# A graph layer's messages held back at the changes of transformer layer, the last block's q moved, and the projection's copies put first on ACT

## The chip, the cores and the metric

The kernel runs on one core of one Trainium2 chip. The metric is the device time of one execution in microseconds (us); the time of a version is the median of its runs. A separate execution is taken by the hardware profiler, and all views come from that one. TensorE is called PE in the views, VectorE DVE, ScalarE ACT, GpSimd POOL; SP issues most of the DMAs.

## The reference

All is fp32. There are 3125 nodes of 256 features and 100,000 edges, sorted by target node (`dst`). Cut to what matters:

```
xn  = layernorm(x)                                   # 3125 x 256
gnn = normalize(relu([xn, h_N] @ W2.T))              # row norm 1
      h_N = segment_sum(relu([xn[src], edge_attr] @ W1.T + b1), dst)
mix = xn; four times:
      h = layernorm(mix)*g1 + b1
      q = softmax(h @ Wq, within a head), k = softmax(h @ Wk, over the nodes), v = h @ Wv
      mix += (q @ (k.T @ v)) @ Wo + bo               # 8 heads of 32
      mix += gelu(layernorm2(mix) @ W1 + b1) @ W2 + b2   # 1024 wide
x   = x + gnn + mix
out = layernorm-ed top-2-of-16 mixture of experts on layernorm(x), plus x
```

The softmax of k runs over all nodes. So k.T @ v of a layer is known only when the last node has been seen, and no q @ (k.T @ v) can start before that: this is what is called a change of layer below.

## The kernel before, in words

The 3125 nodes are 25 tiles of 125 rows (`t`), in 7 blocks of 4, 4, 4, 4, 4, 3 and 2 tiles (`BLOCKS`). All of x stays on the chip as `xm`.

**Prologue** (0 to 126 us). For each block: normalize x (`stage_xn`), scale its rows for layer 0 on ACT (`stage_xh1`, L379, one ACT copy for each tile), transpose it on PE and copy that out on ACT (`stage_xnT`, copy in L389), multiply it with the message weights (`stage_proj`, L399) and write this projection to a table `proj` in memory. Beside that runs the first half of layer 0.

**First half of a layer, by blocks**: `stage_t1` transposes the normalized rows (`hT`); `stage_k` (matmul L432) keeps a running maximum over the nodes (L434, `neg` L443) and takes exponentials on ACT; `stage_q` (matmul L458) is the softmax within heads: maximum `qm` L464, subtraction L465 and, after ACT's exponential, sum L467, reciprocal L468, product L469 on DVE; `stage_ek` and `stage_qT` transpose both (L480, L144), and `stage_m` (L495) adds the block's k.T @ h to `msum`, rescaled on DVE.

**Change of layer**: `context` divides `msum` (`mean`, L516), transposes it (`meanT`, L521, with scale and shift half on ACT, half on DVE), multiplies with Wv (`ctx`, L528; masked on DVE) and Wo (`mo`, L537, L538). `stage_y` (L547) then adds q @ mo to `xm` block by block, with the statistics of the second layernorm; `stage_ln2` normalizes (`xh`, L122) and adds b2 on POOL (L563); `stage_t2` transposes it (`h2T`, L144).

**Second half, by blocks**: `stage_f1` (L581, gelu on ACT) and `stage_f2` (L591). The next layer's k, q, ek, qT and m of block b−1 follow f2 of block b, so that only the last two blocks' are left when the last f2 is done.

**Messages.** 784 chunks of 128 edges make 98 groups of 8. A group has three kinds of steps. Kind 0, `load_chunk`: one indirect DMA on POOL (L255) gathers 128 rows of the table; the first chunk of a group also loads the edge attributes `ea` on SP. Kind 2, `message_step`: 16 matmuls for the attributes (`pw`, L294), four additions on DVE (L298), four relus on ACT (L299), and a matrix `hot` of targets on DVE (L301). Kind 1, `sum_step`: 16 matmuls that sum the group by target (`pq`, L279), a copy on ACT (`osb`, L282), and for the group before two transposes (`win`, L270) that are added to `hNT` (L273).

The steps lie in one list `due`, each with a place: kind 1 of group g at g, kind 2 at g + 0.5, the gathers up to 1.25 groups (`LEAD`) ahead of use. They are mixed into layers 0 to 2: each piece of the transformer's work calls `worked(columns)` (L324) with its number of matmul columns. That advances `place` and emits each step that has come due, a gather after a tiny copy (`tick`, L334) on POOL that waits for that piece of work:

```
place += columns * (NG + 1 + LEAD) / total
while due and due[-1][0] <= place:
    _, kind, step, i = due.pop()
```

`total` is 579,330 columns, so a group is emitted every 5779. `spread` turns this on in the prologue's last blocks. In `context` and after `stage_y` of blocks 0 and 1, five further calls `worked(12 * D)` stand, which are no work of the transformer.

The instructions of PE, ACT and POOL are executed in the order of the program text; those of DVE and SP in an order that a scheduler chose when the kernel was built.

**Last layer.** After layer 2 a branch (L804) chooses another way for targets far apart, which this input doesn't take. Then come the loads of w2x and w2n (L813), and the update of the nodes (`stage_g`, matmuls L617 and L620, squares `sq` L625) is mixed into `context` of the last layer through the same three `worked(12 * D)` calls. Routing and the experts follow.

Of the kernel before, what the change touches and what calls it, by code (L numbers as in the profile page):

```python
# [8 lines left out]
F32 = mybir.dt.float32  # L9
# [8 lines left out]
D = 256  # L18
P = 128
TP = 125  # L20
NT = N // TP
KC = D // P
# [10 lines left out]
DEPTH = 4  # L33
# [6 lines left out]
BT = 4  # L40
# [24 lines left out]
def gps_layer(ctx: ExitStack, tc: tile.TileContext, a, out):  # L65
# [60 lines left out]
    with ExitStack() as ph:  # L126
# [189 lines left out]
        NB = len(BLOCKS)  # L316
        attention = NT * (KC * D + 2 * KC * TP + 3 * KC * P + KC * (D + 1))
        forward = NT * (KC * D + KC * P + NF * KC * TP + NF * D)
        total = (DEPTH - 1) * (attention + forward + 60 * D)
        place = -LEAD  # L320
        spread = False
        tick = tmp.tile([1, 1], F32, name="tick")

        def worked(columns, mark=None):  # L324


            nonlocal place
            if not spread:
                return
            place += columns * (NG + 1 + LEAD) / total  # L330
            while due and due[-1][0] <= place:
                _, kind, step, i = due.pop()
                if kind == 0 and mark is not None:
                    nc.gpsimd.tensor_copy(tick, mark)  # L334
                    mark = None
                step(i)

        def affine(dst, ps, l, which):
            nc.scalar.activation(dst[:, 0, :], ps[:, 0, :], AF.Identity,  # L339
# [18 lines left out]
        def stage_xn(b):  # L358
            r = BLOCKS[b]
            n = len(r)  # L360
            for t in r:
                stats(tmp, xm[:, t, :], t)
            rs = tmp.tile([TP, 3, 2, BT], F32, name="rs", bufs=3)
            st["rs", b] = rs
            v = mv[:, r[0]:r[-1] + 1, 1]
            if n < BT:
                nc.vector.memset(rs[:, 0], 1.0)
            nc.vector.tensor_scalar(rs[:, 0, 0, :n], v, EPS, None, op0=ALU.add)
            nc.vector.scalar_tensor_tensor(rs[:, 0, 1, :n], rs[:, 0, 0, :n], EPS, v, op0=ALU.mult, op1=ALU.add)
            nc.vector.tensor_mul(rs[:, 0, 1, :n], rs[:, 0, 1, :n], rs[:, 0, 0, :n])  # L370
            rsqrt(rs[:, 1], rs[:, 0], rs[:, 2])
            for i, t in enumerate(r):
                nc.vector.tensor_scalar(xm[:, t, :], xm[:, t, :], mv[:, t, 0:1], rs[:, 1, 0, i:i + 1],
                                        op0=ALU.subtract, op1=ALU.mult)
            nc.vector.tensor_mul(rs[:, 2, 0, :], rs[:, 0, 0, :], rs[:, 1, 1, :])
# [129 lines left out]

        def context(l):
            nonlocal mo
            bo = tmp.tile([P, D], F32, name="bo")  # L510
            nc.sync.dma_start(bo, rows_bcast(a["mix_bo"][l], P))
            mean = tmp.tile([P, KC, D], F32, tag="pj", name="mean", bufs=2)
            ksr = tmp.tile([P, KC], F32, name="ksr")
            nc.vector.reciprocal(ksr, msum[:, :, D])
            for c in range(KC):
                nc.vector.tensor_scalar(mean[:, c, :], msum[:, c, :D], ksr[:, c:c + 1], None, op0=ALU.mult)  # L516
            worked(12 * D)
            ps = mm_tile("meanT_ps").rearrange("p (h m) -> p h m", h=KC)
            for h in range(KC):
                for c in range(KC):  # L520
                    nc.tensor.transpose(ps[:, h, c * P:(c + 1) * P], mean[:, c, h * P:(h + 1) * P], ident)  # L521
            meanT = tmp.tile([P, KC, D], F32, tag="pj", name="meanT", bufs=2)
            affine(meanT, ps, l, 0)
            worked(12 * D)
            ps = mm_tile("ctx_ps")[:, :D].rearrange("p (c m) -> p c m", c=KC)
            for c in range(KC):
                for h in range(KC):
                    nc.tensor.matmul(ps[:, c, :], wt["Wv"][:, h, c * P:(c + 1) * P],  # L528
                                     meanT[:, h, c * P:(c + 1) * P],
                                     start=(h == 0), stop=(h == KC - 1))  # L530
            ctxT = tmp.tile([P, KC, P], F32, name="ctxT")
            nc.vector.tensor_mul(ctxT, ps, bmask[:, None, :].to_broadcast([P, KC, P]))
            worked(12 * D)
            ps = mm_tile("mo_ps").rearrange("p (c d) -> p c d", c=KC)
            mo = tmp.tile([P, KC, D], F32, name="mo")
            for c in range(KC):
                nc.tensor.matmul(ps[:, c, :], ctxT[:, c, :], wt["Wo"][:, c, :], start=True, stop=True)  # L537
            nc.vector.scalar_tensor_tensor(mo, bo[:, None, :].to_broadcast([P, KC, D]), 1.0 / HEADS, ps,  # L538
                                           op0=ALU.mult, op1=ALU.add)


        def stage_y(l, b):
# [110 lines left out]
        with tc.manual_schedule(engines=in_order):  # L653

            prepared = windows()
            stage_xn(0)
            stage_xh1(0)
            stage_xnT(0)
            stage_proj(0)
            stage_xn(1)  # L660
            stage_t1(0, 0)
            for b in range(NB + 1):
                if b < NB:
                    stage_k(0, b)
                    if b + 2 < NB:
                        stage_xn(b + 2)
                    stage_q(0, b)
                if b > 1:
                    next(prepared, None)
                if b > 0:  # L670
                    stage_m(0, b - 1)
                if b + 1 < NB:
                    stage_xh1(b + 1)
                    stage_xnT(b + 1)
                    if b > 1:
                        next(prepared, None)
                    stage_proj(b + 1)
                    stage_t1(0, b + 1)
                if b < NB:
                    if b > 1:  # L680
                        next(prepared, None)
                    stage_ek(0, b)
                    stage_qT(0, b)
                if b == NB - 2:
                    for _ in prepared:
                        pass
                    spread = True
            for l in range(last):
                start_layer(l)
                context(l)  # L690
                load(l + 1, "Wk", "Wq", "Wv")
                stage_y(l, 0)
                stage_ln2(0)
                stage_y(l, 1)
                worked(12 * D)
                stage_t2(l, 0)
                worked(12 * D)
                for b in range(NB):
                    stage_f1(l, b)
                    if b > 1:  # L700
                        stage_ek(l + 1, b - 2)
                        stage_qT(l + 1, b - 2)
                    if 0 < b < NB - 1:
                        stage_y(l, b + 1)
                    if b > 1:
                        stage_m(l + 1, b - 2)
                    if b > 0:
                        stage_t1(l + 1, b - 1)
                    if b + 1 < NB:
                        stage_ln2(b + 1)  # L710
                    stage_f2(l, b)
                    stage_stats(b)
                    if b > 0:
                        stage_k(l + 1, b - 1)
                    if b + 1 < NB:
                        stage_t2(l, b + 1)
                    if b > 0:
                        stage_q(l + 1, b - 1)
                    stage_ln1(b)
                stage_ek(l + 1, NB - 2)  # L720
                stage_qT(l + 1, NB - 2)
                stage_t1(l + 1, NB - 1)
                stage_m(l + 1, NB - 2)
                stage_k(l + 1, NB - 1)
                stage_q(l + 1, NB - 1)
                stage_ek(l + 1, NB - 1)
                if l + 1 < last:
                    stage_qT(l + 1, NB - 1)
                    stage_m(l + 1, NB - 1)
            while due:  # L730
                _, _, step, i = due.pop()
                step(i)
            stage_qT(last, NB - 1)
            stage_m(last, NB - 1)

        def any_order():
            table = dram.tile([ROWS, D], F32, name="table")
# [70 lines left out]
        edges_only.close()  # L808
        gates = ph.enter_context(tc.tile_pool(name="gates", bufs=1))
        w2x = wts.tile([P, KC, D], F32, tag="wk", name="w2x")  # L810
        w2n = wts.tile([P, KC, D], F32, tag="wq", name="w2n")
        for w, k in ((w2x, 0), (w2n, D)):
            nc.sync.dma_start(w, a["gnn_W2"][k:k + D].rearrange("(c p) n -> p c n", p=P))  # L813
        gw = gates.tile([P, KC, E], F32, name="gw")
# [117 lines left out]
        with tc.manual_schedule(engines=in_order - {mybir.EngineType.Pool}):  # L932
            start_layer(last)
            load_update(0)
            load_update(1)
            parts = [(0, slice(0, 1)), (0, slice(1, 2)), (1, slice(0, 1))]

            def worked(columns, mark=None):
                if columns == 12 * D and parts:
                    stage_g(*parts.pop(0))  # L940

            context(last)
            stage_y(last, 0)
            stage_ln2(0)
            add_update(0)
            stage_g(1, slice(1, 2))
# [319 lines left out]
```

## Time and profile before

| | us |
|---|---|
| median of 3 runs (lowest, highest) | 2221.84 (2219.28, 2224.5) |
| profiled execution | 1994.73 |
| span in its trace | 1993.0 |
| last projection to first f1 of layer 0 | 126.8 to 179.2 |
| last f2 of layer 0 to first f1 of layer 1 | 529.2 to 595.8 |
| last f2 of layer 1 to first f1 of layer 2 | 942.7 to 1014.7 |
| last f2 of layer 2 to first f1 of layer 3 | 1362.7 to 1418.8 |

The times in all views are counted from the start of the span. The profiled execution is 11% shorter than the runs, and 1.7 us longer than its span. A row of a view names the engine, the line of the kernel and the tiles (out<-in); a wait is put down to the instruction whose end released it.

### The profile page before, as it was taken

The numbers are of one execution on the slowest core, as the hardware profiler recorded it, in microseconds if no ns is written. First come the engines' busy times: TensorE is split into PE (matmuls) and PEld (weight loads), VectorE is DVE, ScalarE is ACT, GpSimd is POOL, SyncE is SP. The second block draws the span as 40 slices with busy tenths as digits, with TensorE's granted clock in tenths as the row PEclk, the third lists the DMA queues.
The fourth block names the chain that finished last, engine by engine and source line by source line (L and its number), as shares of the span: only waits on it lengthen the run. The fifth ranks groups of instructions, "written<-read, shape, count | busy, mean of one in ns | idle before, by whom it ended". The sixth has DMA issues, their size and how long they took to land. (4 is left out here: it accounts for less than half of the span.)

```text
span 1993.0 us, 30766 instructions
## 1 busy us (share of the span) xinstructions
PE 1807.7 (91%) x9749; PEld 1269.3 (64%) x9749; DVE 1165.1 (58%) x3761; ACT 743.6 (37%) x1343; POOL 1126.5 (57%) x1429
## 2 busy tenths in 40 slices
PE   6988999999888999999889999998999994999963
PEld 4764656666655666667546666666777783888841
DVE  7654566666664666766656666765646653333326
ACT  3543444344533444544333444443222231222202
POOL 1026777677667777777677777771114435545512
PEclk9998999999988999999889999999999996999987
DMA  6123333233433233334423233333211113777744
GB/s 188 66 77 92 89 85 88 79 88 93 129 98 91 84 93 91 89 84 127 118 81 89 85 90 87 89 89 100 67 29 29 28 19 116 241 259 260 273 130 120
DMA packets 83294, 210.74 MB, mean 106 GB/s; under 512 B 26523, under 2 KB 42306, under 8 KB 78389
## 3 DMA queue, kind: packets, MB, share of 16 engines
q0 software_dynamic: 44800, 118.16, 20.6%
q1 hardware_dynamic: 37246, 87.31, 13.9%
q10 hardware_dynamic: 1078, 3.20, 0.6%
q8 instruction: 84, 1.38, 0.3%
q14 instruction: 86, 0.70, 0.1%
HBM read 187.34 MB, written 21.19 MB: 105 GB/s over the span
## 5 line engine op out<-in xcount | busy, mean ns | idle before, releaser
L255 POOL DMA_INDIRECT gat<-proj,src_i x784 | 761.9, 972 | 212.4 <-issue 163.4
L581 PE MATMUL f_ps<-h2T,ww 128*128 128x500 f32 (+2 forms) x896 | 360.6, 551 | 6.4 <-ACT h2T L339 5.8
L299 ACT ACTIVATE gat<-gat 128x512 f32<-128x512 f32 x392 | 237.6, 630 | 341.0 <-DVE gat L298 315.4
L591 PE MATMUL f_ps<-ww,gT 128*125 128x256 f32 x1600 | 362.3, 382 | 0.0
L298 DVE TENSOR_TENSOR gat<-gat,pw 128x512 f32<-128x512 f32 x392 | 245.5, 680 | 162.1 <-PE pw L294 138.3
L591 PEld LDWEIGHTS f_ps<-ww,gT 128*125 128x125 f32 x1600 | 295.1, 188 | 58.4 <-issue 10.5
L581 PEld LDWEIGHTS f_ps<-h2T,ww 128*128 128x128 f32 x896 | 167.0, 192 | 168.5 <-issue 122.8
L583 ACT ACTIVATE gT<-f_ps,ffb 128x500 f32<-128x500 f32 (+2 forms) x224 | 135.6, 631 | 136.4 <-PE f_ps L581 135.8
L279 PE MATMUL pq<-gat,hot 128*32 128x256 f32 x1568 | 137.6, 405 | 22.4 <-ACT gat L299 22.3
L273 DVE TENSOR_TENSOR hNT<-hNT,win_ps 128x64 f32 x392 | 84.7, 216 | 74.4 <-PE win_ps L270 64.4
L925 POOL DMA_INDIRECT slots<-rec,at x50 | 59.5, 1189 | 110.0 <-DVE rs_u L113 63.7
L596 DVE TENSOR_TENSOR xm<-xm,f_ps 125x512 f32<-125x512 f32 (+1 forms) x52 | 34.7, 667 | 138.7 <-PE f_ps L591 136.4
L1120 PE MATMUL e_ps<-ew,hs 128*128 128x256 f32 x464 | 112.8, 381 | 2.2 <-DVE o L1124 2.2
L294 PE MATMUL pw<-w1w,ea 4*128 4x256 f32 x1568 | 114.6, 403 | 0.0
L1127 POOL DMA_INDIRECT outs<-o,ids x58 | 57.4, 989 | 100.6 <-DVE o L1125 97.5
L458 PE MATMUL q_ps<-wwq,hT 128*125 128x256 f32 x400 | 99.8, 402 | 4.6 <-DVE gat L298 3.6
L563 POOL TENSOR_TENSOR xm<-xm,b 125x1024 f32<-125x1024 f32 (+2 forms) x28 | 59.9, 2140 | 77.6 <-DVE xh L122 58.5
L547 PE MATMUL y_ps<-mo,qT 128*125 128x256 f32 x400 | 98.0, 397 | 4.9 <-DVE mo L538 4.9
L294 PEld LDWEIGHTS pw<-w1w,ea 4*128 4x128 f32 x1568 | 72.5, 185 | 45.0 <-issue 34.5
L495 PE MATMUL m_ps<-xh,ek 125*128 125x257 f32 x400 | 97.9, 398 | 1.8 <-ACT ek L481 1.8
L279 PEld LDWEIGHTS pq<-gat,hot 128*32 128x32 f32 x1568 | 49.6, 112 | 77.9 <-ACT gat L299 45.3
L1120 PEld LDWEIGHTS e_ps<-ew,hs 128*128 128x128 f32 x464 | 85.2, 190 | 20.4 <-issue 4.5
(222 smaller groups left out, 2652.8 us busy)
## 6 DMA issues: line engine op xcount, KB each, us to landing
ew<-ffn_w SPq DMA_DIRECT2D x37, 1154.0 KB
gat<-proj,src_i POOLq DMA_INDIRECT x784
ww<-mix_W SPq DMA_DIRECT2D x8, 1024.0 KB
ea<-eaT SPq DMA_DIRECT2D x392, 4.0 KB
ogs<-outs SPq DMA_DIRECT2D x6, 448.0 KB
ogs<-outs ACTq DMA_DIRECT2D x6, 448.0 KB
out<-ogs SPq DMA_DIRECT2D x6, 448.0 KB
xnT_d<-stage SPq DMA_DIRECT2D x5, 500.0 KB
```

Source lines behind the costliest of these rows:

```text
L255: nc.gpsimd.indirect_dma_start(out=gats[-1][:, (j // SC) % 2, j % SC, :], out_offset=None, in_=proj, in_offset=bass.IndirectOffsetOnAxis(a ...
L279: nc.tensor.matmul(pq[s * W:(s + 1) * W, :], hot[:, s * SC + i, :], gats[s // 2][:, s % 2, i, :], start=(i == 0), stop=(i == SC - 1))
L294: nc.tensor.matmul(pws[s][:, i, :], ea[s * W:s * W + 4, i * P:(i + 1) * P], w1w[s * W:s * W + 4, :], start=True, stop=True)
L298: nc.vector.tensor_add(msg, msg, pws[s])
L299: nc.scalar.activation(msg, msg, AF.Relu)
L458: nc.tensor.matmul(ps[:, i, :], hT[:, c, cols(o + i)], wt["Wq"][:, c, :], start=(c == 0), stop=(c == KC - 1))
L495: nc.tensor.matmul(ps, st["ek", b][:, i, c * P:(c + 1) * P], xh1s[b % 2][:, i, :], start=(i == 0), stop=(i == n - 1))
L547: nc.tensor.matmul(ps[:, i, :], qT[:, c, cols(t0 + i)], mo[:, c, :], start=(c == 0), stop=(c == KC - 1))
L581: nc.tensor.matmul(ps, wt["W1"][:, c, f * P:(f + 1) * P], st["h2T", b][:, c, :m], start=(c == 0), stop=(c == KC - 1))
L583: nc.scalar.activation(gT[:, f, :m], ps, AF.Gelu, bias=ffb[:, l, f:f + 1])
L591: nc.tensor.matmul(ps[:, i, :], st["gT", b][:, f, cols(o + i)], wt["W2"][:, f, :], start=(f == 0), stop=(f == NF - 1))
L1120: nc.tensor.matmul(ps[:, j, :], x["hs"][:, f, j * P:(j + 1) * P], x["w2"][:, f, :], start=(f == 0), stop=(f == NEF - 1))
```

## The change

Four things are done.

1. *Held steps.* A flag `held` stops `worked` from emitting anything between the last f2 (in layer 0: the last k of the prologue) and the end of `stage_y(l, 0)`. In that stretch a new function `fill(kind)` emits steps at chosen places: up to one message after the last block's layernorm, one sum before the last `stage_m`, one sum after `meanT` and one message after `mo`; none of these in layer 0. The calls `worked(12 * D)` go. `total` becomes 496,536 columns, so that outside these stretches a group is emitted every 4953 columns.
2. *q of the last block.* Its matmuls and softmax move from before the last `stage_m` into `context`, after `mean`; its transposes (`stage_qT`) go behind `stage_y` of block 1 (in the last layer, of block 0). The last but one block's `stage_qT` moves behind k of the last block.
3. *Prologue.* `stage_xnT` comes before `stage_xh1`, so ACT makes the projection's copies first.
4. *Last layer.* `stage_g`'s parts move one place later, q taking the first place; w2n gets a buffer of its own in the pool `gates`, since Wq is still needed, and so its load comes after the branch.

By the built order, the message groups finished at `meanT` of the four changes of layer are 0, 33, 67, 98 before and 0, 33, 66, 98 after. Before `stage_y` of layer 0, 7 gathers are issued before and 1 after. There are 412 ticks before and 387 after, and 784 gathers in both.

```
-        total = (DEPTH - 1) * (attention + forward + 60 * D)
+        at_end = sum(len(r) * (2 * KC * TP + KC * D + 2 * KC * P + KC * (D + 1)) for r in BLOCKS[-2:])
+        total = (DEPTH - 1) * (attention + forward) - (DEPTH - 1) * (at_end + BT * KC * D)
...
-            if not spread:
+            if not spread or held:
                 return
...
+        def fill(kind):
+
+            while due and due[-1][1] in (0, kind):
+                _, k, step, i = due.pop()
+                step(i)
+                if k == kind:
+                    return
...
-        def context(l):
+        def context(l, between):
...
-            worked(12 * D)
+            between[0]()
             ps = mm_tile("meanT_ps").rearrange("p (h m) -> p h m", h=KC)
...
-            worked(12 * D)
+            between[1]()
             ps = mm_tile("ctx_ps")[:, :D].rearrange("p (c m) -> p c m", c=KC)
...
-            worked(12 * D)
+            between[2]()
             ps = mm_tile("mo_ps").rearrange("p (c d) -> p c d", c=KC)
...
+            between[3]()
...
+            stage_xnT(0)
             stage_xh1(0)
-            stage_xnT(0)
...
                 if b + 1 < NB:
+                    stage_xnT(b + 1)
                     stage_xh1(b + 1)
-                    stage_xnT(b + 1)
...
             for l in range(last):
                 start_layer(l)
-                context(l)
+                more = (lambda kind: None) if l == 0 else fill
+                context(l, [lambda: stage_q(l, NB - 1), lambda: more(1), lambda: None, lambda: more(2)])
                 load(l + 1, "Wk", "Wq", "Wv")
                 stage_y(l, 0)
+                held = False
                 stage_ln2(0)
                 stage_y(l, 1)
-                worked(12 * D)
+                stage_qT(l, NB - 1)
                 stage_t2(l, 0)
-                worked(12 * D)
...
+                    if b == NB - 1:
+                        stage_ln1(b)
+                        held = True
+                        fill(2)
...
                 stage_ek(l + 1, NB - 2)
-                stage_qT(l + 1, NB - 2)
                 stage_t1(l + 1, NB - 1)
                 stage_m(l + 1, NB - 2)
                 stage_k(l + 1, NB - 1)
-                stage_q(l + 1, NB - 1)
+                stage_qT(l + 1, NB - 2)
                 stage_ek(l + 1, NB - 1)
-                if l + 1 < last:
-                    stage_qT(l + 1, NB - 1)
-                    stage_m(l + 1, NB - 1)
+                fill(1)
+                stage_m(l + 1, NB - 1)
...
-        w2n = wts.tile([P, KC, D], F32, tag="wq", name="w2n")
+        w2n = gates.tile([P, KC, D], F32, name="w2n")
...
-            context(last)
+            context(last, [lambda: stage_q(last, NB - 1), lambda: stage_g(0, slice(0, 1)),
+                           lambda: stage_g(0, slice(1, 2)), lambda: stage_g(1, slice(0, 1))])
             stage_y(last, 0)
+            stage_qT(last, NB - 1)
```

More of the change, by code (lines that the diff above doesn't have):

```diff
@@ L661, in gps_layer @@
             stage_t1(0, 0)
[L662 to L666, printed above, removed]
+            for b in range(NB):
+                stage_k(0, b)
+                if b + 2 < NB:
+                    stage_xn(b + 2)
+                if b < NB - 1:
                     stage_q(0, b)
+                else:
+                    held = True
                 if b > 1:
@@ L678, in gps_layer @@
                     stage_t1(0, b + 1)
[L679 to L682, printed above, removed]
+                if b > 1:
+                    next(prepared, None)
+                stage_ek(0, b)
+                if b < NB - 1:
                     stage_qT(0, b)
@@ L687, in gps_layer @@
                     spread = True
+            stage_m(0, NB - 1)
             for l in range(last):
                 start_layer(l)
-                context(l)
+                more = (lambda kind: None) if l == 0 else fill
+                context(l, [lambda: stage_q(l, NB - 1), lambda: more(1), lambda: None, lambda: more(2)])
                 load(l + 1, "Wk", "Wq", "Wv")
                 stage_y(l, 0)
+                held = False
                 stage_ln2(0)
                 stage_y(l, 1)
-                worked(12 * D)
+                stage_qT(l, NB - 1)
                 stage_t2(l, 0)
-                worked(12 * D)
                 for b in range(NB):
@@ L712, in gps_layer @@
                     stage_stats(b)
+                    if b == NB - 1:
+                        stage_ln1(b)
+                        held = True
+                        fill(2)
                     if b > 0:
@@ L718, in gps_layer @@
                         stage_q(l + 1, b - 1)
-                    stage_ln1(b)
+                    if b < NB - 1:
+                        stage_ln1(b)
                 stage_ek(l + 1, NB - 2)
-                stage_qT(l + 1, NB - 2)
                 stage_t1(l + 1, NB - 1)
@@ L732, in gps_layer @@
                 step(i)
-            stage_qT(last, NB - 1)
-            stage_m(last, NB - 1)
         def any_order():
@@ L935, in gps_layer @@
             load_update(1)
-            parts = [(0, slice(0, 1)), (0, slice(1, 2)), (1, slice(0, 1))]
             def worked(columns, mark=None):
-                if columns == 12 * D and parts:
-                    stage_g(*parts.pop(0))
-            context(last)
+                pass
+            context(last, [lambda: stage_q(last, NB - 1), lambda: stage_g(0, slice(0, 1)),
+                           lambda: stage_g(0, slice(1, 2)), lambda: stage_g(1, slice(0, 1))])
             stage_y(last, 0)
+            stage_qT(last, NB - 1)
             stage_ln2(0)
```

## The prediction

> **What bounds the kernel now.** I read the page's first rows, then a table of windows by stage, the waits, and the timeline at the changes of layer. "T0" to "T3" below are the stretches from the last f2 (for T0, the last projection) to the next f1.
>
> Section 1 of the page, and the table of windows (columns: window, its length, then busy time of each engine, PEclk, DMA share, GB/s):
> ```profile
> PE 1807.7 (91%) x9749; PEld 1269.3 (64%) x9749; DVE 1165.1 (58%) x3761; ACT 743.6 (37%) x1343; POOL 1126.5 (57%) x1429
> ...
> 126.00:182.00 56.00, 41.80 (x226) 27.81 (x225) 28.83 (x86) 16.54 (x31) 33.22 (x42) 0.82 0.36 105
> 182.00:529.00 347.00, 336.45 (x1991) 223.24 (x1990) 213.45 (x638) 155.30 (x272) 254.76 (x354) 0.99 0.32 91
> 529.00:606.00 77.00, 60.52 (x370) 37.87 (x369) 53.40 (x168) 29.42 (x54) 49.39 (x65) 0.88 0.38 109
> 940.00:1020.00 80.00, 64.53 (x363) 40.24 (x362) 52.39 (x163) 28.96 (x53) 51.46 (x65) 0.85 0.37 107
> 1345.00:1420.00 75.00, 63.02 (x331) 51.85 (x328) 43.37 (x141) 21.91 (x41) 12.67 (x21) 0.95 0.31 92
> ```
> See two regimes. Inside a layer (182 to 529) TensorE is busy 336 of 347 us at clock 0.99. In the changes of layer it idles 14.2, 16.5, 15.5 and 12.0 us (length minus PE) and its clock drops. The change can win at most this idle time, 58 us, and what the low clock costs.
>
> Who makes it idle, from the waits (us in total, times, longest):
> ```profile
> PE qT_ps L144 <- DVE qs L469: 24.6, 8, 4.9
> PE pq L279 <- ACT gat L299: 22.3, 16, 3.9
> PE h2T_ps L144 <- DVE xh L122: 7.7, 4, 3.5
> PE proj_ps L399 <- ACT stage L389: 6.9, 7, 3.9
> PE y_ps L547 <- DVE mo L538: 4.9, 4, 2.1
> ...
> POOL tick L334 <- DVE neg L443: 130.7, 4, 126.3
> ```
> The first two rows are what the change aims at: q's transposes wait for q's softmax, and the sums of a group placed in these stretches wait for its own messages (message and sum stand too close there). The last row: POOL does nothing until the first gather at 133.
>
> The low clock, from TensorE's timeline in T1 (start, length; the bracket is the idle time before):
> ```profile
> 574.43 6.64 PE L547 MATMUL y_ps<-mo,qT 128*125 128x256 f32 x16 [2.09 <-DVE mo L538]
> ...
> 582.22 3.72 PE L547 MATMUL y_ps<-mo,qT 128*125 128x256 f32 x16
> ```
> The same 16 matmuls take 6.64 us after gaps and 3.72 after steady work.
>
> **What the Trainium skill says.** "TensorE: Matmul & The Clock Gate", Part 1: The HAM clock gate: the array falls to half rate after an idle window of about 3.4 us and comes back after one of sustained work. The trace agrees: 6.64 against 3.72, after gaps of 2.1 to 4.9 us in T1. So a gap costs its length and some slow work behind it. The same page's "Architectural detail" gives ScalarE, VectorE and GpSimdE short queues in strict order; the trace agrees in that four gather-adds of 2.47 us run ahead of q's first maximum at 538.4. "DMA: Bandwidth & Descriptors", Anatomy of one DMA (SWDGE path), puts about 2.0 us of fixed cost on such a DMA; the shortest distance from the end of a gather on POOL to its add is here 1.9 us. "Perfetto Trace Analysis", Optimization Strategy, advises interleaving regimes; the change does the opposite in T0 to T3, so the fill taken out must be worth less there than the gaps it caused.
>
> **The change part by part.** A group's steps cost TensorE 1.15 (pw) + 1.07 (pq) + 0.38 (win) = 2.6 us at full clock. They do not vanish: taken out of T, they are paid in the steady stretches. So I compare each T after with T before *less the groups moved out*. Chains below are sums of timeline durations plus the gaps I expect.
>
> *T1* (529.2 to 595.8 = 66.6 us, 6 groups = 15.6). After: 2 groups; 10.4 moved, base 56.2. Work left: k 2.7+1.9, q 2.8+1.9, m 2.8+1.9, ek, hT and qT about 2.8, two groups 5.2, meanT, ctx, mo 2.1, y 7.4, h2T 1.4, together 34 (rounded up for joints). Gaps: ek 3.3 (the held-back fill puts four gather-adds on DVE before k's maximum), m 1.3, ek 1.2, ctx 3.2 (meanT's affine is serial over ACT and DVE, and on DVE stands behind qm and sub of the moved q), mo 0.9, h2T 4.0 (two adds, statistics, normalization of the first block; no fill stands in front), f1 1.4: 15.3. Sum 49.3. Slow clock: before it cost 66.6 − 44.4 work − 16.5 idle = 5.7 here, 11.9 in T2; the last gaps (3 to 4 us) stay, I take 6. **55.3 against 56.2: −1.**
>
> *T2* (71.9; 6 pq and 5.75 pw, after 1 and 2: 11.6 moved, base 60.3). As T1 less the first 1.5 and some gap: 47 + 6. **−7.**
>
> *T0* (126.8 to 179.2 = 52.4, three groups = 7.8 moved, base 44.6). After: no group at all; gaps 0.8, 0.8, 2.0, 2.2, 0.8, 1.0, h2T 3.4, f1 1.4; f1 near 161.3, so 34.5, and 4 for clock. **−6.**
>
> *T3* (1362.7 to 1418.8 = 56.1; 1.8 moved, base 54.3). The update's matmuls (L617, L620) move one place later; q's softmax hides behind meanT, but six squares for the update (`sq`, L625, 0.41 us each) now stand after y's adds on DVE, so h2T waits about 5.7 instead of 1.1. 56 to 58. **+3.** The w2n load, now issued after the branch, has its first reader (L620) behind q, meanT and L617, some 4 us; it can't gain, being issued later; bounds 0 and +4, taken as 0 because before the same wait on the branch cost L617 1.15.
>
> *Prologue.* ACT copied four scaled tiles (1.69 us from 34.50) before the projection's two (from 36.09); the projection waited 3.91 us at 36.7 and 1.19 at 13.2. Swapped, each wait falls by at most 1.7: −1.2 and −1.5 = **−2.5** rounded. The four scaled copies come 1 us later, ahead of hT, for which TensorE has 16 projection matmuls (5.4 us): hidden.
>
> *Steady stretches.* `total` falls from 579,330 to 496,536, so a group comes every 4953 columns instead of 5779. Before, a group took about 12.35 us there, 9.75 of it other work; after 9.75 × 4953/5779 + 2.6 = 10.95. POOL needs for a group 8 gathers at 1.25 (row after row) to 1.30 (with a tick copy), 10.2 with half of them ticked, and 0.6 of L563's adds (59.9/98): 10.8. Page rows:
> ```profile
> L255 POOL DMA_INDIRECT gat<-proj,src_i x784 | 761.9, 972 | 212.4 <-issue 163.4
> ...
> L563 POOL TENSOR_TENSOR xm<-xm,b 125x1024 f32<-125x1024 f32 (+2 forms) x28 | 59.9, 2140 | 77.6 <-DVE xh L122 58.5
> ```
> This just fits, but in layer 0 only one gather is issued before y, then L563's add waits for xh, so the gathers start at 161 instead of 133 and 22 of them lose their cover. Eight gathers and the landing end near 173; the first gather-add stands in DVE's order near 166. That is some 7 us late, taken back in part: **+4**. Bounds: −10 (the 25 us that PE idles in the three steady stretches fall by 40% as fill gets denser) and +30 (see (a)). The moved steps' DVE work (2.6 adds, 0.9 win adds, 0.4 hot) and ACT's (four of 0.63) lie beside TensorE: in 182 to 529 DVE is busy 61%, ACT 45%, and a group every 10.95 us raises that to some 66 and 50%. SP issues a group's four `ea` loads in 1.3 us, and waits 912 us in all for pw to free their buffers, so it is not the limit; the next layer's Wq, whose buffer the moved q frees later, has a layer's time to land.
>
> Sum: −1 −7 −6 +3 −2.5 +4 = −9.5, i.e. 1985 for the profiled execution (1994.7; its span 1993.0). The median of the runs, 2221.84, is 227 us above that execution; no view says where, so I don't scale: **2212**.
>
> **Rivals.**
> (a) *Slower: POOL becomes the bound.* If a group costs POOL over 10.95, every excess accumulates: adds wait on DVE in order, pq waits on PE. For: 57% POOL share already, starved start, tick copies, adds held behind xh. Against: before, the gathers were mostly 5 to 9 us early, and 25 ticks fewer are needed (387 for 412). At 11.2 us per group: 0.25 × 94 = 24 − 13.5 = +10, 2232. It decides from about 11.1.
> (b) *Larger gain.* With the waits for q and for fresh messages gone (first two wait rows, 47 us) the clock hardly drops: 5 less in T1 and T2, 3 in T0; and h2T waits only 2, as in before, three times 2 less: −9.5 − 19 = −28.5, 2193. For: those two rows are the longest. Against: DVE's chain from y to xh is not shorter, and no fill is left in it.
> (c) *Nothing.* The fill was good cover; without it the DVE and ACT chains show as new gaps of the same length, and the late first gathers eat the prologue's gain: within 0.2%. T3 speaks for it.
> That the copies' swap does nothing, since ACT is free in time anyway, is excluded by the 1.69 us ahead of the copy.
>
> **How the numbers follow.** A measurement of this kernel can tell about 0.2% (4.4 us) from no change. My forecast (−5 to −20) 0.5; (b) 0.15; (c) 0.13; (a) 0.22. Faster by over 0.2%: 0.65; within: 0.13; slower: 0.22. Range: down to 2190, a little past (b); up to 2234, (a) with its price slightly exceeded; outside it lie a POOL delay over 25 us and a gain over 32.
>
> **What would show it.** In the profile after: no `qT_ps <- qs` and no `pq <- gat` waits over 1 us in T1 and T2; T0 near 35 to 39 us long, T1 near 55, T2 near 53, T3 56 to 58; `h2T_ps <- xh` grown to about 4 us each; the wait at the projection down by 2.5; POOL back to back after 161; steady stretches 30 us longer in all by the groups moved in, and PE's idle there not above 35 us. Idle above that on `gat <- DMA` or POOL would show (a); T1 and T2 near 45 would show (b). The forecast is wrong if the steady stretches grow by more than 45 us.

## The result, and the profile after

The changed kernel takes 2258.4 us (median of 4 runs, 2257.78 to 2264.11); the kernel before took 2223.17 beside it. The ratio is 1.0167, 95% interval 1.0145 to 1.0189: slower by 1.7%, outside my range and on the other side.

The profiled execution after has a span of 2257.0 us, the one before that the prediction was read from 1993.0. That pair can't be compared: run e1 below profiled the unchanged kernel again and found 2211.1, which agrees with its runs. **The execution that I read was 10% shorter than an ordinary one, and what it lacked decides this case.** (The 11% given ahead is what the runs are longer by.) All that follows compares ordinary executions.

First row of the page, and the table of windows of the changed kernel (window, length, busy time of PE, PEld, DVE, ACT, POOL, then PEclk, DMA share, GB/s), cut at the changes of layer:

```profile
PE 1952.2 (86%) x9749; PEld 1335.9 (59%) x9749; DVE 1178.6 (52%) x3761; ACT 743.7 (33%) x1343; POOL 1118.8 (50%) x1404
...
124.00:159.00 35.00, 26.00 (x113) 19.86 (x112) 18.28 (x64) 6.39 (x15) 2.48 (x3) 0.88 0.18 53
159.00:616.00 457.00, 407.55 (x2130) 256.29 (x2130) 230.11 (x669) 168.92 (x294) 295.88 (x406) 0.91 0.28 80
616.00:676.00 60.00, 41.30 (x204) 30.43 (x202) 36.11 (x115) 15.44 (x30) 14.12 (x15) 0.78 0.22 67
1630.00:1685.00 55.00, 45.58 (x206) 38.26 (x205) 35.44 (x134) 10.69 (x23) 7.59 (x12) 0.94 0.31 94
```

The same of the kernel before, in the ordinary execution (run e1):

```profile
PE 1909.8 (86%) x9749; PEld 1314.5 (59%) x9749; DVE 1169.3 (53%) x3761; ACT 745.0 (34%) x1343; POOL 1122.5 (51%) x1429
...
125.00:188.00 63.00, 37.51 (x217) 25.79 (x216) 28.43 (x83) 14.91 (x29) 31.26 (x40) 0.77 0.29 85
188.00:600.00 412.00, 368.18 (x1994) 237.73 (x1995) 215.65 (x642) 157.51 (x274) 256.38 (x357) 0.93 0.27 77
600.00:685.00 85.00, 58.25 (x338) 37.21 (x340) 46.97 (x151) 24.19 (x46) 40.97 (x56) 0.78 0.29 85
1582.00:1638.00 56.00, 45.78 (x218) 38.30 (x218) 34.21 (x123) 13.87 (x26) 6.24 (x12) 0.94 0.29 90
```

The changes of layer did get shorter (63 to 35, 85 to 60), and the layers longer (412 to 457). In whole sums, from the ends of the last f2 and the starts of the first f1 in both traces:

| us | before (e1) | after | difference |
|---|---|---|---|
| prologue | 125.0 | 123.7 | −1.3 |
| T0, T1, T2, T3 | 62.8, 85.1, 85.0, 56.5 | 35.6, 60.2, 60.2, 54.4 | −79.0 |
| layers 0, 1, 2 between them | 412.5, 405.8, 405.7 | 456.7, 448.5, 445.6 | +126.8 |
| last layer and experts | 572.7 | 572.2 | −0.5 |

13 groups moved into the layers (82 sums of groups there before, 95 after). They cost 126.8 / 13 = 9.8 us each where I had priced 2.6. In time for each group of eight gathers that start in them, the layers are alike: 1224.0 us for 84.8 groups before, 1350.8 for 94.7 after, 14.4 and 14.3 us each, though the pace was set to 17% denser. It looks as if something in the layers lets a group through in 14 us and no faster.

What is it? The waits of the changed kernel (us in total, times, longest), PE's first, then from all engines:

```profile
PE pq L279 <- issue: 21.7, 25, 4.1
...
PE pw L294 <- issue: 18.4, 26, 2.5
...
PE h2T_ps L144 <- DVE xh L122: 12.9, 4, 3.9
```

```profile
ACT osb L282 <- remote: 168.9, 25, 11.6
POOL tick L336 <- DVE neg L453: 139.6, 7, 122.3
```

"issue" is a wait that nothing in the profile explains, "remote" one that a signal ended whose sender the profile does not tell. In the first execution pw's row had no idle time at all, and PE, DVE and ACT had no "remote" wait (of over 0.15 us); in e1 such waits add up to 202 us, in the changed kernel to 385. One such place in PE's timeline (start, length, then the idle time before):

```profile
199.87 0.39 PE L279 MATMUL pq<-gat,hot 128*32 128x256 f32 x1 [0.24 <-issue]
201.29 0.38 PE L279 MATMUL pq<-gat,hot 128*32 128x256 f32 x1 [1.03 <-issue]
202.00 0.39 PE L279 MATMUL pq<-gat,hot 128*32 128x256 f32 x1 [0.33 <-issue]
202.71 0.38 PE L279 MATMUL pq<-gat,hot 128*32 128x256 f32 x1 [0.32 <-issue]
```

and POOL's timeline just before it (the gathers run on at 199.90 and 201.15):

```profile
194.90 0.94 POOL L255 DMA_INDIRECT gat<-proj,src_i  x1 [0.30 <-issue]
196.15 0.95 POOL L255 DMA_INDIRECT gat<-proj,src_i  x1 [0.30 <-issue]
197.40 0.95 POOL L255 DMA_INDIRECT gat<-proj,src_i  x1 [0.30 <-issue]
198.65 0.94 POOL L255 DMA_INDIRECT gat<-proj,src_i  x1 [0.30 <-issue]
```

Matmuls of one group, for which the profile finds no wait, come 0.7 or 1.4 us apart, in a run of gathers 1.25 us apart. I counted in layers 0 to 2, without the changes between them, how much PE idled in each microsecond, by the number of gathers started in the 16 us before:

| gathers in 16 us | 8 | 9 | 10 | 11 |
|---|---|---|---|---|
| changed kernel, PE idle | 5% | 6% | 14% | 27% |
| kernel before, e1 | 5% | 7% | 11% | 29% |
| execution first shown | 2% | 2% | 2% | 4% |

The faster the gathers have just run, the more PE stands still, except in the execution first shown. Late data is no explanation: the waits that end with a gather's landing (DVE and ACT, `gat <- DMA`) come to 45.5 us in the execution first shown, 31.5 in e1 and 26.3 in the changed kernel. All this is a correlation; the experiments turn it into a cause.

### The profile page after: what moved, and what is told of

Its sections match the earlier page's. It is cut to its first block, busy times and chain, and to the rows that moved or that the text cites. A ratio compares the mean times of both kernels' runs of the same rounds, so it can differ in the third digit from the quotient of the medians.

```text
span 2257.0 us, 30731 instructions
## 1 busy us (share of the span) xinstructions
PE 1952.2 (86%) x9749; PEld 1335.9 (59%) x9749; DVE 1178.6 (52%) x3761; ACT 743.7 (33%) x1343; POOL 1118.8 (50%) x1404
## 3 DMA queue, kind: packets, MB, share of 16 engines
q1 hardware_dynamic: 37246, 87.31, 12.4%
## 5 line engine op out<-in xcount | busy, mean ns | idle before, releaser
L602 PE MATMUL f_ps<-ww,gT 128*125 128x256 f32 x1600 | 385.1, 397 | 13.9 <-issue 5.9
L592 PE MATMUL f_ps<-h2T,ww 128*128 128x500 f32 (+2 forms) x896 | 370.3, 562 | 12.4 <-ACT h2T L349 7.9
L602 PEld LDWEIGHTS f_ps<-ww,gT 128*125 128x125 f32 x1600 | 307.7, 196 | 84.4 <-issue 21.7
L279 PE MATMUL pq<-gat,hot 128*32 128x256 f32 x1568 | 163.7, 408 | 39.6 <-issue 21.7
L294 PE MATMUL pw<-w1w,ea 4*128 4x256 f32 x1568 | 152.9, 433 | 42.8 <-issue 18.4
L294 PEld LDWEIGHTS pw<-w1w,ea 4*128 4x128 f32 x1568 | 90.7, 197 | 104.0 <-issue 60.5
L282 ACT COPY osb<-pq 128x256 f32<-128x256 f32 x98 | 36.4, 371 | 303.4 <-remote 168.9
L279 PEld LDWEIGHTS pq<-gat,hot 128*32 128x32 f32 x1568 | 57.2, 112 | 115.2 <-issue 57.8
L301 DVE TENSOR_TENSOR hot<-slot,drel 128x256 f32<-128x256 f32 x98 | 52.9, 540 | 137.0 <-remote 77.4
L558 PE MATMUL y_ps<-mo,qT 128*125 128x256 f32 x400 | 111.5, 436 | 4.9 <-issue 4.1
```

Of the source, the lines that this page charges most:

```text
L279: nc.tensor.matmul(pq[s * W:(s + 1) * W, :], hot[:, s * SC + i, :], gats[s // 2][:, s % 2, i, :], start=(i == 0), stop=(i == SC - 1))
L294: nc.tensor.matmul(pws[s][:, i, :], ea[s * W:s * W + 4, i * P:(i + 1) * P], w1w[s * W:s * W + 4, :], start=True, stop=True)
L558: nc.tensor.matmul(ps[:, i, :], qT[:, c, cols(t0 + i)], mo[:, c, :], start=(c == 0), stop=(c == KC - 1))
L592: nc.tensor.matmul(ps, wt["W1"][:, c, f * P:(f + 1) * P], st["h2T", b][:, c, :m], start=(c == 0), stop=(c == KC - 1))
L602: nc.tensor.matmul(ps[:, i, :], st["gT", b][:, f, cols(o + i)], wt["W2"][:, f, :], start=(f == 0), stop=(f == NF - 1))
```

## The experiments

Ratios are to the kernel before, run beside each.

**First set: is the execution typical, and which part costs?** e1 is the kernel before. e2 has only the prologue's two swaps. e3 has only `held`, `fill` and the new `total`; e4 only the move of q and w2n, with the old `total` and the five `worked(12 * D)`.

> The kernel before, unchanged, for a profile of an ordinary execution of it. If the 227 us between the runs and the profiled execution shown are an ordinary matter of stalls that that execution escaped, the new profile has a span near 2220 us, PE idle over 200 us (144 in the profile shown), with idle of 'issue' and 'remote' kind inside the layers, as the changed kernel's profile has. If the runs carry time outside the span, the span is near 1993 again.

> Only the order of the copies in the prologue is changed. My sum: -2.5 us, about 2220. If the ACT copies delay hT and so k (k_ps <- hT waits 4.5 us in the changed kernel's prologue), 0 to +2.

> The held steps, the fills and the denser pace alone; q stays in its place, the prologue's order as before, w2n as before. Theory 'steady': the loss comes from more steps for each column inside the layers; then this alone is slower by 30 us or more, near 2255. Rival 'q': the loss comes from q's softmax ahead of meanT; then this is within 10 us of 2222.

> The move of q, its transposes and w2n alone; the pace, the calls that fill the changes of layer and the prologue's order as before. Theory 'steady': 2210 to 2225 (the waits for q, 24.6 us in all, go in part). Rival 'q': slower by 20 us or more.

| | median us | ratio, 95% |
|---|---|---|
| e1 | 2211.97 | 1.0008 (0.9994 to 1.0022), span 2211.1, PE idle 260.6 |
| e2 | 2208.77 | 1.0001 (0.9984 to 1.0018) |
| e3 | 2269.63 | 1.0284 (1.0252 to 1.0315) |
| e4 | 2203.15 | 0.9962 (0.9941 to 0.9982) |

The time that the first execution lacked, 218 us between the two spans, lay inside the span, in the stretches with messages: prologue, T3 and the rest are as long in e1 as in the first execution (within 2.5 us), the layers 58 to 63 us longer each, T0 to T2 11 to 19. The held steps alone, with their denser pace, lose 2.8%, more than the whole change; q's move gains 0.4%; the prologue's swap gains nothing that these times can tell. (PE idle is counted from its first matmul to its last; it was 144 us in the execution first shown.)

**Second set: gathers or steps, pace or hold?** e5 and e6 leave the gathers out of the kernel before and of the changed one, so that the messages lack the gathered rows:

```
-            nc.gpsimd.indirect_dma_start(
...
-                nc.vector.tensor_add(msg, msg, pws[s])
+                nc.vector.tensor_add(msg, fixed, pws[s])     # fixed: zeros
```

e7 and e8 change the pace alone:

```
-        total = (DEPTH - 1) * (attention + forward + 60 * D)
+        total = 496536                                                  # e7, on before
+        total = (DEPTH - 1) * (attention + forward + 120 * D)           # e8, on e4,
+            worked(24 * D)                                              # at all five places
```

> The kernel before with the 784 gathers left out; the messages are added to a tile of zeros, so every other step stays, POOL's ticks too. Theory 'gathers': the stalls in the stretches with messages belong to the gathers; then the three layers fall from 412, 406 and 406 us to about 350 each, as in the execution shown at first, and the total to 1985 to 2010. Theory 'steps': the stalls belong to the steps on PE, DVE and ACT; then 2150 or more.

> The changed kernel with the same left out. 'Gathers': with a group's price back at 2.6 us the emptied changes of layer win: 15 to 45 us less than the kernel before without gathers. 'Steps': still 30 us or more above it.

> The kernel before with the denser pace alone (total 496536), nothing held: groups run out in layer 2's second half. Layers 0 and 1 should then be near the changed kernel's 457 and 448 us if the price of a group there is 10 us whatever is held, with layer 2 that much shorter and the total within 10 us of before (a linear price). If stalls grow faster than the density, the total is slower by 15 us or more. If the pace is harmless and the hold is what hurts, layers 0 and 1 grow by less than 15 us each.

> The kernel with q moved (no hold), with the five fills at a change of layer doubled (24*D columns each) and the pace thinned to match: about 7 groups more go from the layers to the three changes. If a group costs 9.8 us inside a layer and 6.1 in a change of layer, as the changed kernel against the one before says, this gains 7 x 3.7 = 26 us over the kernel with q moved: near 2177. If the changes of layer are full already, 0 or slower.

| | median us | ratio, 95% |
|---|---|---|
| e5 | 1960.17 | 0.8824 (0.8799 to 0.8848) |
| e6 | 1959.87 | 0.8822 (0.8792 to 0.8852) |
| e7 | 2317.85 | 1.0433 (1.0406 to 1.0461) |
| e8 | 2246.31 | 1.0110 (1.0078 to 1.0142) |

Without gathers the two kernels are equal within the noise of two runs each: the loss needs the gathers. There T0 to T3 fall from 237.7 to 183.1 us and the layers grow from 1030.2 to 1079.0, 3.8 us for each of 13 groups. Layer 0 of the changed kernel, without gathers:

```profile
159.00:516.00 357.00, 351.13 (x2130) 230.73 (x2130) 226.43 (x669) 168.09 (x293) 38.02 (x142) 0.99 0.02 6
```

The same 2130 matmul records fill 457 us with them. e7 shows that a denser pace without any hold costs even more: layers 0 and 1 took 468 and 458 us (14.2 us for a gathered group again), the changes of layer grew to 76, 103 and 91, and layer 2 gave back only 41. e8, my try at a better version, missed: the changes of layer swelled from 62, 78 and 85 to 94, 112 and 127 us. A call of 24*D columns lets nearly a whole group out at one place; that such bursts do the harm there is an inference.

The row of pw's matmuls is a handy gauge, since they wait for little (busy, mean | idle before them and what ended it). In e1:

```profile
L294 PE MATMUL pw<-w1w,ea 4*128 4x256 f32 x1568 | 137.8, 420 | 18.2 <-issue 11.7 <-ACT ek L481 3.5 <-ACT gT L583 2.7
```

In the changed kernel:

```profile
L294 PE MATMUL pw<-w1w,ea 4*128 4x256 f32 x1568 | 152.9, 433 | 42.8 <-issue 18.4 <-remote 7.9 <-ACT ek L491 6.1
```

And in e6, the changed kernel without gathers:

```profile
L293 PE MATMUL pw<-w1w,ea 4*128 4x256 f32 x1568 | 117.5, 403 | 0.2 <-issue 0.2
```

The same 1568 matmuls idle 18, 43 and 0.2 us, and their busy time grows with it. Neither e5 nor e6 has a "remote" wait.

**Third set: rate, number or bytes?** e9 and e10 leave out every second pair of gathers; e11 gathers rows of half the length, and the messages lack them; e12 puts time between gathers, on e4:

```
+            if j // SC % 2:                    # e9 (changed kernel), e10 (before)
+                return
...
+                in_=proj.rearrange("n (e d) -> (n e) d", e=2),       # e11 (changed kernel)
...
+            nc.gpsimd.memset(gap_, 0.0)        # e12, after each gather; gap_: 128 x 512
```

> The changed kernel with every second pair of gathers left out (392 of 784; those messages are added to zeros), all other steps kept. Theory 'rate': gathers stall the other engines only where they come faster than about one in 1.75 us (a group of 8 in 14 us, as in all versions so far); with 4 to a group they need 7 us of the 11 and the time is near that without gathers, 1960 to 2020. Theory 'fixed price': each gather costs the others 303/784 = 0.39 us; then 1960 + 152 = 2112.

> The kernel before with the same left out. 'Rate': 1960 to 2010, within 20 us of the changed kernel so treated, so that the hold's loss is gone with the excess rate. 'Fixed price': 1960 + 392 x 0.32 = 2085.

> The changed kernel with all 784 gathers, but each of 128 rows of 512 bytes instead of 1024 (the messages are then added to zeros over them, so that all waits stay). If the limit is in bytes: as with half the gathers, 2020 or less. If it is in gathers or rows: 2200 or more.

> The kernel with q moved (no hold), and after each gather POOL clears a tile of 128 x 512, which keeps two gathers at least some 1.6 us apart. 'Rate' in the form that bursts make the stalls: PE's idle no longer rises with the number of gathers just before it, and 10 to 40 us less than with q moved alone. If the mean rate alone counts: within 10 us of it. If the gathers come late: slower, with waits of the adds for gathers.

| | median us | ratio, 95% |
|---|---|---|
| e9 | 1967.84 | 0.8893 (0.8869 to 0.8916) |
| e10 | 1969.38 | 0.8900 (0.8873 to 0.8926) |
| e11 | 2235.04 | 1.0100 (1.0064 to 1.0136) |
| e12 | 2184.95 | 0.9872 (0.9852 to 0.9893) |

"Fixed price" falls: half of the gathers cost 8 to 9 us by the medians or some 16 by the ratios (this set ran beside a faster "before"), not 125 or 152, and the loss of the hold is gone. "Rate" is left, and the fourth set says in what sense. Half of the bytes take 0.7% off the changed kernel, by the two ratios: the limit counts gathers or rows, not bytes. Spacing helps, by about 0.9% over e4 by the two ratios. POOL's timeline in e12 has a gather each 1.68 us, 1.76 to 1.79 with a tick; a group then takes POOL 14.4 us and POOL is the bound (DVE's adds wait 223 us for gathers), while pw's idle in the layers is down from 15.5 us in e4 to 3.1, and the "remote" waits from 221 us to none.

**Fourth set: how close may gathers come, and does spacing heal the hold?** The clearing of e12 with 512, 256 or 128 columns, on the changed kernel (e13, e14, e17) and on e4 (e15, e16 with 384, e18):

```
+        gap_ = edge.tile([P, 256], F32, name="gap_", bufs=1)
...
+            nc.gpsimd.memset(gap_, 0.0)
```

> The changed kernel with the clearing of 128 x 512 after each gather. 'Lost gather time': POOL needs 14.4 us for a group, 94.7 groups must run inside the three layers: 1364 us, with 156 for the three changes of layer, 124, 54 and 572 for the rest 2270. 'Bursts only': near the kernel with q moved and spaced, 2185.

> The same with a clearing of 128 x 256: two gathers are then some 1.42 to 1.5 us apart, 12.4 us for a group. If that is slow enough not to stall the others: 94.7 x 12.4 = 1174 in the layers, 2080 in all. If the limit is one in 1.75 us: as without it, 2240 or more.

> The kernel with q moved and a clearing of 128 x 256. If 1.42 to 1.5 us is slow enough: 2 us less for each of 84 groups in the layers than with 512, near 2020. If the limit is one in 1.75 us: as with q moved alone, 2200.

> The kernel with q moved and a clearing of 128 x 384, 1.56 to 1.65 us apart. If slow enough: 1 us less for each of 84 groups than with 512, near 2100. If the limit is one in 1.75 us: between 2185 and 2200.

> The changed kernel with a clearing of 128 x 128 after each gather: some 1.35 us between gathers, 11.5 us for a group. If that doesn't stall the others: 94.7 x 11.6 = 1100 in the layers, 140 in the changes of layer, 749 beside them: 1990. If the limit lies above 1.35 us: stalls come back, 2150 or more.

> The kernel with q moved and the same clearing. Unstalled: 350 us a layer as in the execution shown at first, 190 for the changes of layer: 1990 to 2000, so that the hold ends within 10 us of it, on the side that my sum said. If the limit lies above 1.35 us: 2100 or more, less than the changed kernel.

| clearing | median start to start | q moved alone (e4) | changed kernel |
|---|---|---|---|
| none | 1.29 | 0.9962 (0.9941 to 0.9982) | 1.0167 (1.0145 to 1.0189) |
| 128 | 1.44 | e18: 2163.51, 0.9788 (0.9766 to 0.9810) | e17: 2188.27, 0.9913 (0.9879 to 0.9947) |
| 256 | 1.55 | **e15: 2039.21, 0.9212 (0.9185 to 0.9240)** | e14: 2112.91, 0.9554 (0.9528 to 0.9581) |
| 384 | 1.66 | e16: 2105.92, 0.9521 (0.9492 to 0.9550) | not run |
| 512 | 1.76 | e12: 2184.95, 0.9872 (0.9852 to 0.9893) | e13: 2261.86, 1.0223 (1.0196 to 1.0251) |

From 512 to 256 the times fall as POOL's need for a group does: expected at 2270, 2080, 2020 and 2100, e13 to e16 came out at 2262, 2113, 2039 and 2106. At 128 I expected 1990 for both unless the stalls come back, and they came back. The "remote" waits of PE, DVE and ACT tell it apart most sharply:

| clearing | median start to start | "remote", q moved alone | "remote", changed kernel |
|---|---|---|---|
| none | 1.29 | 221 | 385 |
| 128 | 1.44 | 172 | 197 |
| 256 | 1.55 | 4.5 | 0 |
| 384 | 1.66 | 0 | not run |
| 512 | 1.76 | 0 | 0 |

So the stalls set in between the spacing of the second row (the middle half of the gathers starts 1.36 to 1.48 us after the one before) and that of the third (1.47 to 1.58). It is the spacing in an unbroken series of gathers that counts, not the mean rate: over the layers e15's gathers come oftener (1.62 us apart on average) than e1's (1.81). Nor is it the distance of two alone: in e9 43% of the gathers of layers 0 to 2 still follow within 1.4 us, but seldom more than two in a row, and its "remote" waits are 14 us. POOL in e15, where pw idles 1.0 us in all:

```profile
300.57 0.98 POOL L256 DMA_INDIRECT gat<-proj,src_i  x1 [0.17 <-issue]
301.56 0.33 POOL L259 MEMSET gap__157<- 128x256 f32 x1
302.05 0.95 POOL L256 DMA_INDIRECT gat<-proj,src_i  x1 [0.16 <-issue]
302.99 0.33 POOL L259 MEMSET gap__157<- 128x256 f32 x1
```

and layer 0 in its table of windows:

```profile
181.00:545.00 364.00, 346.96 (x1994) 228.19 (x1994) 217.37 (x641) 156.91 (x274) 322.80 (x583) 0.96 0.30 87
```

364 us where e1 needs 412, with POOL busy 323 instead of 256: a POOL that does more makes the kernel 8% faster. **e15 beats both kernels.** Late gathers are no rival here: e15 waits longer for their landing (86 us) than e4 (29). The hold loses in every row of the table of times. In the rows of 256 and 512 I take it that this is lost gather time: with POOL at 12.4 or 14.4 us for a group, the changes T0 to T2 (139 us in e14) pass with hardly a gather, and POOL can't catch up in layers where PE, by e6, would need 11.4. The traces fit that: the layers take 13.0 us for a gathered group in e14 and in e15, and e14 has 94 to gather there, e15 84. No run tests it alone.

## Why the prediction was wrong

**The step that failed is the price of a group in the steady stretches**: 1.15 + 1.07 + 0.38 = 2.6 us, and a gather stream that "just fits" at 10.8 of 10.95 us. The durations were right for the execution that I read; what was missing is what gathers at 1.25 to 1.30 us do to the others in an ordinary one. Moved groups were to cost 31.6 + 4 us, and cost 126.8, 9.8 us each, well past the 45 us that I had named as the sign of being wrong. Even without gathers they cost 48.8, 3.8 us each (e5, e6), so the price was too low there too; the rest came with the gathers. The first error had a second behind it: I saw that the runs were 227 us longer than the execution I read, said that no view tells where, and built every price on that execution. PE idled 144 us in it and 261 in e1, so the gaps that I priced from it were too small for the runs.

**The changes of layer.** T0: 38.5 forecast, 35.6 measured; its gap before h2T was forecast at 3.4:

```profile
156.82 1.76 PE L144 MATMUL h2T_ps<-ident,xh 125*128 125x125 f32 x8 [3.92 <-DVE xh L122]
```

T1 and T2: 55.3 and 53 forecast, 60.2 each measured. Without gathers (e6) they are 44.1 and 50.5, so the work and the gaps were estimated too high, and the stalls added more. One place in T1 shows how:

```profile
620.76 2.75 PE L468 MATMUL q_ps<-wwq,hT 128*125 128x256 f32 x12
...
629.74 0.69 DVE L474 TENSOR_REDUCE qm<-q_ps 125x16 f32<-125x512 f32 x1 [4.83 <-remote]
...
636.12 0.86 ACT L491 COPY ek<-ek_ps 125x512 f32<-125x512 f32 x2 [2.19 <-remote]
636.76 5.51 PE L505 MATMUL m_ps<-xh,ek 125*128 125x257 f32 x12 [9.47 <-ACT ek L491]
```

By the profile q's matmuls end at 623.5 and PE goes on with other work; yet DVE, idle since 624.9, starts on their result at 629.74, ACT's copy of ek waits in its turn, and then PE waits 9.47 us for ek. POOL starts 13 gathers 1.24 to 1.33 us apart from 617.5 to 632.6. In e6 the same m starts 8.7 us earlier, counted from the group's sum before it. It looks as if the signals between the engines came late; that is a reading of this place, not tested.

T3: 56 to 58 forecast, a loss of 3; 54.4 measured, 2 less than before. h2T waited 3.5 us and not 5.7: six squares do stand behind y's adds on DVE, but they take 2.1 us from 1671.3 to 1673.4.

**Against e1, T0 to T3 became 79 us shorter, where I had 31.6 of moved groups and 11 of gain, and rival (b) 30 of gain**: in an ordinary execution the fills at a change of layer are dear too. So the sign of this part was right and its size too small; the layers took back more.

**Prologue.** −2.5 forecast, −1.3 between e1 and the changed kernel. One pair says little: the prologue took 124.9 to 129.1 us in the 12 profiled executions without the swap, 126.6 on average, and 123.1 to 125.6 in the 8 with it, 124.2 on average. That is some −2.3, near the forecast, and too little for e2's run times (1.0001, give or take 0.0017). The waits were not as forecast, though: the projection's fell from 6.9 to 3.7 us, but k's for hT in the first block rose from 2.5 (first execution) to 4.5, so the cover that I named for the later scaled copies was too thin there.

**POOL's late start.** Gathers to start at 161: 160.46 measured, and the first add at 171.6 where I had 173:

```profile
157.82 2.35 POOL L574 TENSOR_TENSOR xm<-xm,b 125x1024 f32<-125x1024 f32 x1 [26.46 <-DVE rstd L114]
...
160.46 1.00 POOL L255 DMA_INDIRECT gat<-proj,src_i  x1 [0.16 <-issue]
```

**Rival (a)** had the sign and the place, not the mechanism. POOL was no bound in the changed kernel: it was busy 296 of layer 0's 457 us and waited for ticks. It is the bound in e13 (busy 87 to 91% of each layer), where the sum by POOL's need, 2270, came within 9 us. **Rival (c)** describes the kernel without its gathers: e5 and e6 are equal, so that what the order gains, 54.6 us in T0 to T3 and 3.4 in the prologue, is given back, most of it in the layers (48.8). My −9.5 looks too favourable even there: the medians differ by 0.3 us and the two profiled spans by 5.5, with two runs each.

## What to carry to other kernels

Before pricing anything from a profiled execution, hold its span against the runs: if they differ by 10%, the prices belong to another kind of execution, and the first thing wanted is a profile that agrees with the runs. Moving background work out of the gaps into the busy stretches is not paid at its busy time: look at how its rate changes, and what else that rate touches. When a stream of DMAs stalls engines that don't wait for it, try to slow the stream: here one small clearing after each gather brought 8%. Its width has an optimum: 128 columns brought 2%, 256 brought 8%, 512 brought 1%.

## What the runs showed of the hardware

- Indirect gathers of 128 rows issued by POOL every 1.25 to 1.30 us stalled PE, DVE and ACT, in waits that did not end with a gather's landing: with none of the 784 the kernel before took 1960 us, with 392 of them 1969, with all 2212. In series 1.36 to 1.48 us apart (e17, e18) the stalls remained, in series 1.47 to 1.58 us apart (e14, e15) the "remote" waits were gone to within 4.5 us.
- Rows of 512 bytes stalled nearly as much as rows of 1024 (1.0100 against 1.0167 of the kernel before; "remote" waits 298 us against 385).
- The execution first shown had the same spacing (median 1.29 us, and over the layers 1.54 on average, closer than in any other run) and no such stall. So close gathers were needed for the stalls here but were not enough. What set that execution apart, by what way a gather stalls another engine, and whether POOL's instruction or the transfers that it starts do it, no view shows and no run here settles.
